# When a planner frees PSUM banks, how it ranks additions, and where three small loads are issued, in a float32 stack of attention and MLP blocks

## The chip, the cores and the metric

One core of one Trainium2 chip runs the whole program. The metric is device time in microseconds (us), the median of several executions; smaller is better. A profile is one further execution, with every instruction's start and length.

## The reference, cut to what matters

Everything is float32. `x` is 4 x 512 x 512 (four batches of 512 tokens, width 512), the context is 4 x 64 x 512. Four blocks follow one another; cut down:

```
x = x + cross_attention(ln(x), ctx)          # L0, twice: 16 heads of 128, one extra key/value each
x = x + gelu(ln(x) @ w_fc1 + b) @ w_fc2 + b  # L0's MLP, inner width 2048
x = x + alpha * (softmax(x wq (ctx wk)^T / sqrt(512)) (ctx wv)) wo        # L1
h = concat(ctx, x);  a = attention(q=x, kv=h, mask on the ctx part)       # L2, 16 heads of 32
x = x + mlp(rmsnorm(a @ out_w + out_b + x))
x = x + attention(ln(x), ctx, mask) @ cproj_w + b                         # L3, 16 heads of 32
x = x + mlp(ln(x))
```

`alpha` is one number, L2's mask is 4 x 64 int32, L3's mask is 4 x 64 bool. Neither mask is trivial to the program: each becomes an additive term (`mterm2`, `mterm3`) that is 0 or a very large negative number.

## The kernel before, in words

**No instruction's place is written by hand.** The builder functions (`l0_keys`, `l0_values`, `l0_attention`, `mlp`, `l2_attention` and so on) only describe operations to a `Plan`: which engine or engines could do each (`pe`, `dve`, `act`, `pool`, `either` = ACT or DVE, `added` = DVE or POOL), a duration estimated from the element count, and which buffers it reads and writes. `Plan.issue` then works out one order for each engine, before anything runs, and emits the instructions in it. On the chip each engine goes through its own list strictly in order; an instruction that waits for a semaphore holds everything behind it on its engine.

**Memory.** SBUF has one arena of 24 blocks, PSUM eight banks of 512 columns; a `Buf` gets its place when the plan starts the operation that first writes it, and gives it back when the last user in the plan has ended. Constants are "held" buffers with a fixed place. Names in the profile: `arena` is any SBUF buffer, `banks` any bank.

**How the work is split.** The matrix products follow a seven-product scheme (Strassen-Winograd): a 2 x 2 block product is made by seven products instead of eight, with additions of operands before (`moving_sums`, `stationary_sums`, `pair_sums`, `token_sums`, `width_sums`) and of results after. The additions before are `added` operations, one line in the profile (L1048), on DVE or POOL. The results are taken out of the banks by DVE or ACT ("evictions"): L1108 (`plus` of the MLP's first product), L1147 and L1154 (sums of the second), L938 (`plus` in L0's attention), L575/L576 (plain copies on ACT/DVE), L1594 (the exponential of L2's scores, read straight from four banks by ACT), L1388, L1404, L1676. A matmul into a bank must wait until the eviction of what was there is done.

**The order (`merge`, then `attempt`).** Work is recorded in thirteen regions, and in each two or three streams run beside each other (for instance one pair's MLP beside another pair's attention). `merge` interleaves them: `PACES` has for each stream 17 numbers; number k says where the stream should stand, in per cent of the region, when k/16 of its TensorE work is gone, and the stream with the lowest number goes next. This gives each operation a number `n` and a position `pos` (TensorE time before it). `attempt` is a list scheduler over estimated time: whenever an engine is free, it takes from that engine's heap the ready operation with the lowest `n`, if its buffers fit and its `pos` is not further than `AHEAD` (loads: `AHEAD_LOAD`) past the oldest unfinished one. ACT prefers an operation that needs no other activation table, unless one that does is over 6 us earlier in position. An eviction's bank is free, in the plan, at the very moment the eviction ends; its dependents are ready `AFTER` = 0.06 us later, or `AFTER_PE` = 0.2 us after TensorE, plus `BEFORE_PE` = 0.1 us for a TensorE operation.

**The start.** Ahead of the plan, ACT's queue issues the DMAs of `cols` and `alpha` (L663, L665), POOL's the two masks, each broadcast to 128 partitions (L668, L670). All loads of the plan go through SP's queue (L701), in the planned order. L2's context part makes `mterm2` from `mk_i`; L3's makes `mterm3` from `mk_b`; L1's attention uses `alpha` as a scalar.

Line numbers that the text uses further: L717 the products of context and weights (`mm4`), L877 the pair products of `l0_values`, L933 L0's score products, L1089 the MLP's seven products, L1367 the half-width seven products, L1571 L2's scores (four 32-row products into four banks), L1628 the transposes of their exponentials, L1763 the last transposes, before the store.

Of the kernel before, what the change touches and what calls it, by code (L numbers as in the profile page):

```python
# [18 lines left out]
P = 128  # L19
# [58 lines left out]
class View:  # L78
# [5 lines left out]
    def __init__(self, buf, key=None, path=()):  # L84
        self.buf, self.key, self.path = buf, key, path
# [122 lines left out]


class Op:  # L210
    __slots__ = ("n", "pos", "engines", "calls", "wait", "next", "takes", "uses", "table", "ready", "start", "on", "load", "port")


class Plan:
# [8 lines left out]
    SHARED_DVE, SHARED_POOL = 0.45, 0.15  # L223
    BEGIN = {"PE": 1.0, "DVE": 3.0, "ACT": 3.0, "POOL": 3.2, "SP": 0.8}

    def __init__(self, sbuf, ahead, ahead_load, reserve, full, patience, near, paces):
        self.reserve, self.full = reserve, full * BLOCK
        self.sbuf = Memory(BLOCK, sbuf)
        self.psum = Memory(1024, 4)
        self.ahead, self.ahead_load = ahead, ahead_load  # L230
        self.patience, self.near, self.paces = patience, near, paces
        self.ops, self.regions = [], []
        self.pos = 0.0

# [70 lines left out]
    def merge(self):  # L305
# [68 lines left out]
        for n, op in enumerate(merged):  # L374
            op.n, op.pos = n, pos
            pos += op.engines.get("PE", 0.0)

    def order(self):


        self.merge()
        waits = [op.wait for op in self.ops]
        left = {id(b): (b, b.left) for op in self.ops for b in op.uses}
        narrow = []
        while True:
            for op, n in zip(self.ops, waits):
                op.wait = n
            for b, n in left.values():
                b.left, b.at = n, None
            self.sbuf.reset()  # L390
            self.psum.reset()
            out, at = self.attempt(narrow)
            if out:
                return out
            width = 100 + 100 * sum(lo <= at <= hi for lo, hi in narrow)
            if width > 1500:
                raise RuntimeError(f"no room at {at}: {self.sbuf.free}, {self.psum.free}")
            narrow.append((at - width, at + 50))

    def attempt(self, narrow):  # L400
        heaps = {e: [] for e in ("PE", "DVE", "ACT", "POOL", "SP")}
        free_at = dict(self.BEGIN)
        table = None
        dma_free = 0.0
        port_busy = False
        events = [(at, 0, -1) for at in free_at.values()]
        heapq.heapify(events)
# [1 line left out]
        begun = [False] * len(self.ops)  # L409
        oldest = 0  # L410
        now = 0.0
        out = []
        busy = dict.fromkeys(heaps, 0.0)

        def arm(op):
            for e in op.engines:
                heapq.heappush(heaps[e], (op.n, op))

        for op in self.ops:
            op.ready = 0.0  # L420
# [3 lines left out]
        while left:  # L424
            progress = True
            while progress:
# [8 lines left out]
                for e, heap in heaps.items():  # L435
# [3 lines left out]
                    choice = None  # L439
                    second = None  # L440
                    while heap and len(skipped) < 60:
                        n, op = heapq.heappop(heap)
                        if begun[n]:
                            continue
                        skipped.append((n, op))
                        if op.ready > now + 1e-9:
                            continue
                        if op.pos > limit + (ahead_load if op.load else ahead):
                            break
                        room = True  # L450
                        for m in (self.sbuf, self.psum):
                            need = [b for b in op.takes if b.mem is m and b.at is None]
# [13 lines left out]
                            continue  # L466
                        choice = op
                        break
                    if second is not None and (choice is None or choice.pos > second.pos + 6.0):
                        choice = second  # L470
                    for n, op in skipped:
                        if op is not choice:
                            heapq.heappush(heap, (n, op))
                    if choice is None:
                        continue
                    op = choice
# [31 lines left out]
            now = events[0][0]  # L508
            while events and events[0][0] <= now + 1e-9:
                _, kind, n = heapq.heappop(events)  # L510
                if kind != 1:
                    continue
                op = self.ops[n]
# [2 lines left out]
                for b in op.uses:  # L516
                    b.left -= 1
                    if b.left == 0:
                        b.mem.give(b)
                for o in op.next:  # L520
                    o.wait -= 1
                    at = now + (self.AFTER_PE if op.on == "PE" else self.AFTER)
# [125 lines left out]
def stack(nc, const, sbuf, psum, a, out):  # L648
# [12 lines left out]
    nc.gpsimd.memset(eps[:, 1:2], 1e-6)  # L661
    cols = const.tile([P, NCOL], FP, name="cols")
    nc.scalar.dma_start(out=cols, in_=a["cols"])  # L663
    alpha = const.tile([P, 1], FP, name="alpha")
    nc.scalar.dma_start(out=alpha, in_=a["alpha"].to_broadcast([P, 1]))  # L665

    mk_i = const.tile([P, B * T], I32, name="mk_i")
    nc.gpsimd.dma_start(out=mk_i, in_=a["mask_i"].to_broadcast([P, B * T]))  # L668
    mk_b = const.tile([P, B * T], U8, name="mk_b")
    nc.gpsimd.dma_start(out=mk_b, in_=a["mask_b"].to_broadcast([P, B * T]))  # L670
    pl = Plan(BLOCKS, AHEAD, AHEAD_LOAD, RESERVE, FULL, PATIENCE, NEAR, PACES)
    sb, ps = pl.sb, pl.ps
    ctxT = pl.held(const.tile([P, NC * B * T], FP, name="ctxT")).v(NC, B * T)
    mterm2, mterm3 = (pl.held(const.tile([P, B * T], FP, name=f"mterm{i}")).v(B, T) for i in (2, 3))

    def col(name, i=None):
        lo, hi = _COL_AT[name]
# [6 lines left out]
    def dve(n):  # L684
        return pl.op(DVE=t_dve(n))
# [801 lines left out]
    def l2_context():  # L1487
# [4 lines left out]
            o.tensor_copy(apart[:, :256].k(0), row[:, :256])  # L1492
        with pool(256) as o:
            o.tensor_tensor(apart[:, 256:].k(1), row[:, 256:], row[:, :256], ALU.subtract)
        with dve(256) as o:
            o.tensor_scalar(mterm2, mk_i.rearrange("p (b s) -> p b s", b=B), 0.0, -3.0e38, ALU.is_equal, ALU.mult)
        bias_steps("L2_xattn_q_b")
        bias_steps("L2_k_b")
        shared2.update(row=apart, ckT=context_keys(2, "L2_k_b"), cv=context_values(2, row))
# [188 lines left out]

    def l3_context():
        row = load_row("L3_xattn_v_b")  # L1690
        with dve(256) as o:
            o.tensor_scalar(mterm3, mk_b.rearrange("p (b s) -> p b s", b=B), 0.0, LOWEST, ALU.is_equal, ALU.mult)
        bias_steps("L3_xattn_q_b")
        shared3.update(ckT=context_keys(3, "L3_xattn_k_b"), cv=context_values(3, row))

# [122 lines left out]
    g = {}  # L1818

    def a0():  # L1820
        l1.append(l1_project())
        l2_context()

# [5 lines left out]
    def a3(pair):  # L1829
# [18 lines left out]


BLOCK, BLOCKS = 8 * KW, 24  # L1850
AHEAD, AHEAD_LOAD, RESERVE = 170.0, 90.0, 2
FULL = 24


PATIENCE, NEAR = 7.0, 37.0

PACES = [
    [
        [2, 7, 11, 22, 33, 23, 51, 60, 57, 66, 72, 60, 77, 83, 93, 101, 104],
        [-4, 6, 18, 24, 27, 26, 37, 42, 48, 66, 62, 76, 74, 81, 86, 92, 97],  # L1860
        [-1, 1, 14, 14, 28, 38, 37, 50, 54, 53, 61, 74, 76, 83, 90, 96, 111],
    ],
    [
        [-1, 8, 26, 23, 26, 28, 35, 43, 60, 61, 72, 61, 72, 72, 77, 79, 88],
        [18, 28, 34, 25, 39, 34, 60, 34, 55, 62, 73, 70, 77, 98, 92, 102, 111],
    ],
    [
        [4, 13, 16, 19, 27, 36, 40, 46, 37, 58, 68, 63, 67, 76, 86, 86, 87],
        [-8, 1, 9, 15, 22, 26, 34, 41, 50, 52, 51, 64, 71, 73, 83, 88, 95],
        [-1, -2, 3, -2, 8, 6, 38, 42, 54, 74, 71, 76, 81, 88, 93, 111, 109],  # L1870
    ],
    [
        [-13, -5, 2, 16, 27, 26, 31, 24, 39, 48, 49, 55, 57, 63, 80, 95, 109],
        [-4, 10, 18, 19, 26, 43, 41, 56, 54, 61, 73, 73, 75, 94, 91, 95, 96],
    ],
    [
        [2, 5, 12, 19, 16, 36, 37, 50, 47, 54, 62, 79, 73, 80, 89, 96, 103],
        [1, 5, 12, 14, 24, 28, 38, 46, 54, 59, 62, 82, 84, 87, 84, 83, 86],
        [8, 24, 24, 32, 38, 48, 51, 61, 68, 60, 49, 62, 89, 97, 102, 104, 100],
    ],  # L1880
    [
        [-7, 9, 23, 34, 46, 63, 48, 45, 55, 75, 68, 63, 82, 78, 104, 102, 107],
        [7, 19, 26, 39, 37, 54, 56, 60, 54, 51, 76, 75, 68, 86, 97, 115, 120],
    ],
    [
        [-44, -40, -30, -8, -3, -1, 6, 16, 25, 16, 30, 43, 49, 54, 65, 75, 84],
        [-2, 4, -1, 16, 22, 37, 57, 53, 60, 67, 60, 77, 83, 62, 66, 81, 87],
        [-2, 11, 20, 17, 33, 50, 47, 53, 57, 49, 65, 77, 75, 89, 89, 98, 101],
    ],
    [  # L1890
        [-1, 4, 8, 6, 10, 20, 39, 44, 34, 44, 64, 44, 54, 60, 70, 67, 84],
        [2, 8, 10, 10, 36, 41, 64, 77, 76, 77, 84, 100, 109, 83, 90, 85, 106],
    ],
    [
        [-3, -10, 13, 23, 31, 33, 19, 44, 51, 56, 63, 67, 66, 74, 84, 102, 115],
        [23, 10, 19, -11, 18, 26, 41, 50, 50, 48, 52, 54, 63, 67, 76, 82, 87],
    ],
    [
        [3, 7, 13, 19, 24, 29, 34, 39, 45, 54, 63, 69, 74, 79, 85, 91, 97],
        [0, 6, 13, 19, 25, 31, 39, 45, 51, 57, 64, 69, 75, 81, 88, 94, 100],  # L1900
    ],
    [
        [-6, 0, 7, 12, 17, 22, 30, 36, 43, 49, 57, 63, 67, 73, 77, 85, 93],
        [-2, 3, 11, 19, 25, 31, 38, 44, 51, 56, 63, 69, 75, 81, 88, 94, 93],
        [0, 12, 13, 19, 24, 29, 35, 51, 45, 41, 49, 57, 76, 80, 83, 93, 96],
    ],
    [
        [-17, 8, 2, -1, 6, 42, 42, 48, 16, 18, 42, 59, 81, 93, 90, 99, 103],
        [-6, -5, 5, 15, 26, 36, 50, 40, 46, 53, 42, 53, 64, 80, 85, 84, 99],
    ],  # L1910
    [
        [-30, -33, -25, -10, 17, 3, 23, 46, 59, 48, 56, 45, 58, 65, 76, 73, 82],
        [-14, -3, 8, -8, 25, 53, 31, 5, 5, 26, 40, 52, 63, 75, 74, 54, 76],
    ],
]

# [55 lines left out]
```

## Time and profile before

| what | value |
|---|---|
| median of 3 runs | 2750.61 us (2749.08 to 2750.61) |
| the profiled execution | 2748.76 us, span of its instructions 2747.0 us |
| TensorE (PE) busy | 2701.2 us, 98% |
| VectorE (DVE) busy | 2044.7 us, 74% |
| GpSimd (POOL) busy | 1323.0 us, 48% |
| ScalarE (ACT) busy | 931.5 us, 34% |
| granted TensorE clock | 1.000 |
| DMA | 164.06 MB, mean 60 GB/s |

How to read the views. The page gives busy time of each engine and the costliest groups of instructions: line, engine, operation, output<-input, shape and count, then busy time, mean length of one in ns, and the idle time of the engine just before them with what ended it. The wait table says who waited for whom. The table by stretch gives each engine's busy time in a stretch of the span. In the time-ordered list a row is: start, us, engine, line, operation, count, and in brackets the idle time before it and what ended that. Matmuls are pipelined and their ends are modelled, so a matmul's row can cover up to about 0.2 us in which TensorE in fact stood still; distances between the starts of matmuls are the surer measure.

### The profile page before, as it was taken

What the parts mean: (1) busy time and instruction counts of PE and PEld (TensorE: products, weight loads), DVE (VectorE), ACT (ScalarE), POOL (GpSimd) and SP (SyncE); (2) the same over time, 40 slices, a digit from 0 to 9 for tenths busy, and PEclk for the clock granted to TensorE, in tenths of its full rate; (3) what the DMA queues carried; (4) which work ended last, traced back from release to release, by engine and by line L of the source; (5) the groups of instructions that cost most, each with busy time, mean ns of one, the idle gap of its engine ahead of it and who ended that gap; (6) DMA issues with size and microseconds to landing.
All of it is one profiled execution on the core that took longest, in us unless ns stands there. A gap on an engine that the chain in (4) does not pass through costs nothing. (4 is left out here: it accounts for less than half of the span.)

```text
span 2747.0 us, 34916 instructions
## 1 busy us (share of the span) xinstructions
PE 2701.2 (98%) x12012; PEld 1648.4 (60%) x12012; DVE 2044.7 (74%) x3661; ACT 931.5 (34%) x1759; POOL 1323.0 (48%) x1465
## 2 busy tenths in 40 slices
PE   8999999999999999999999999999999999999999
PEld 6877778788854455556555665555544545454444
DVE  6788778786864577776787678687877878878655
ACT  3223242142331114453463255154523223333211
POOL 5567576574842262333335232424745485646421
PEclk9999999999999999999999999999999999999999
DMA  7222423243121020010102011110211120202200
GB/s 242 84 89 81 131 77 115 64 134 93 50 62 57 16 69 20 20 59 14 44 25 88 8 31 45 56 32 24 70 50 35 41 67 20 58 8 84 77 16 31
DMA packets 230368, 164.06 MB, mean 60 GB/s; under 512 B 9088, under 2 KB 198656, under 8 KB 230192
## 3 DMA queue, kind: packets, MB, share of 16 engines
q1 hardware_dynamic: 229824, 161.52, 19.4%
q8 instruction: 96, 1.57, 0.2%
q14 instruction: 80, 0.66, 0.1%
q0 software_dynamic: 80, 0.16, 0.0%
q10 hardware_dynamic: 288, 0.15, 0.0%
HBM read 157.60 MB, written 4.19 MB: 59 GB/s over the span
## 5 line engine op out<-in xcount | busy, mean ns | idle before, releaser
L1048 POOL TENSOR_TENSOR arena<-arena 128x256 f32<-128x256 f32 (+4 forms) x1016 | 1064.1, 1064 | 970.5 <-DVE arena L576 169.8
L1089 PE MATMUL banks<-arena 128*128 128x512 f32 x2688 | 1201.9, 594 | 7.9 <-DVE arena L1108 2.6
L1089 PEld LDWEIGHTS banks<-arena 128*128 128x128 f32 x2688 | 497.8, 190 | 578.3 <-issue 497.6
L1048 DVE TENSOR_TENSOR arena<-arena 128x256 f32<-128x256 f32 (+4 forms) x664 | 574.1, 879 | 89.9 <-POOL arena L1048 24.8
L575 ACT COPY arena<-banks 128x512 f32<-128x512 f32 (+4 forms) x563 | 280.5, 516 | 793.9 <-PE banks L1089 196.3
L1367 PE MATMUL banks<-arena 128*128 128x256 f32 x1792 | 408.3, 380 | 3.2 <-DVE arena L938 1.5
L1367 PEld LDWEIGHTS banks<-arena 128*128 128x128 f32 x1792 | 336.2, 190 | 79.8 <-issue 21.9
L576 DVE COPY arena<-banks 128x512 f32<-128x512 f32 (+2 forms) x353 | 213.1, 613 | 160.2 <-PE banks L1089 52.5
L1124 ACT ACTIVATE arena<-arena,cols 128x512 f32<-128x512 f32 x192 | 138.0, 722 | 313.2 <-DVE arena L1048 172.9
L1108 DVE TENSOR_TENSOR arena<-banks,arena 128x512 f32<-128x512 f32 x240 | 163.8, 685 | 90.6 <-PE banks L1089 76.2
L933 PE MATMUL banks<-arena 128*128 128x260 f32 x896 | 212.0, 385 | 0.3 <-DVE arena L938 0.2
L1594 ACT ACTIVATE arena<-banks,arena 128x512 f32<-128x512 f32 x256 | 174.7, 687 | 95.1 <-DVE arena L1584 49.5
L933 PEld LDWEIGHTS banks<-arena 128*128 128x128 f32 x896 | 163.5, 188 | 36.0 <-ACT arena L575 3.0
L1582 DVE TENSOR_REDUCE arena<-banks 128x1 f32<-128x512 f32 x256 | 167.5, 681 | 13.3 <-PE banks L1571 12.2
L717 PE MATMUL banks<-ctxT,arena 128*128 128x128 f32 (+1 forms) x1152 | 164.1, 292 | 12.1 <-DMA arena<-in_L_wv 6.5
L717 PEld LDWEIGHTS banks<-ctxT,arena 128*128 128x128 f32 x1152 | 148.8, 194 | 29.5 <-issue 11.2
L1628 PEld LDWEIGHTS banks<-ident,arena 128*128 128x128 f32 x1024 | 116.5, 141 | 81.6 <-issue 35.1
L1628 PE MATMUL banks<-ident,arena 128*128 128x128 f32 x1024 | 140.9, 276 | 3.5 <-ACT arena L1594 2.9
L717 PE MATMUL banks<-arena 128*128 128x512 f32 (+2 forms) x432 | 140.4, 482 | 0.0
L1147 DVE TENSOR_TENSOR arena<-banks,arena 128x512 f32<-128x512 f32 x144 | 98.2, 685 | 50.2 <-PE banks L1089 50.1
L1605 POOL TENSOR_TENSOR arena<-arena 128x256 f32<-128x256 f32 x64 | 39.5, 617 | 188.6 <-DVE arena L1584 160.2
L717 PEld LDWEIGHTS banks<-arena 128*128 128x128 f32 x432 | 72.4, 191 | 68.3 <-issue 65.7
(155 smaller groups left out, 2528.4 us busy)
## 6 DMA issues: line engine op xcount, KB each, us to landing
arena<-in_L_w SPq DMA_DIRECT2D x192, 256.0 KB, 3.3
arena<-in_L_wk SPq DMA_DIRECT2D x80, 256.0 KB, 4.9
arena<-in_L_wv SPq DMA_DIRECT2D x64, 256.0 KB, 5.6
arena<-in_L_wqT SPq DMA_DIRECT2D x64, 256.0 KB, 5.5
arena<-in_L_wo SPq DMA_DIRECT2D x64, 256.0 KB, 5.7
arena<-in_L_wq SPq DMA_DIRECT2D x32, 256.0 KB, 3.3
arena<-in_L_wo SPq DMA_DIRECT2D x8, 1024.0 KB, 5.4
arena<-in_L_wv SPq DMA_DIRECT2D x6, 1024.0 KB, 5.7
```

The lines of the kernel that those rows point to most:

```text
L575: "ACT": lambda e, out, in_: e.copy(out, in_),
L576: "DVE": lambda e, out, in_: e.tensor_copy(out, in_),
L717: o.matmul(dst, lhs(c), rhs(c), start=(c == 0), stop=(c == NC - 1))
L933: o.matmul(p[:, : 2 * KP], lhs(c), rhs(c, b % 2), start=(c == 0), stop=(c == 1))
L1048: o.tensor_tensor(out, x, y, op)
L1089: o.matmul(p.v(), lhs(c), rhs(c), start=(c == 0), stop=(c == 1))
L1108: o.tensor_tensor(t.v(), p.v(), y.v(), ALU.add)
L1124: o.activation(g[f].v(), src.v(), func, bias=col(b1, q * NC + f))
L1367: o.matmul(p[:, i * 256 : (i + 1) * 256], lhs(c), rhs(c), start=(c == 0), stop=(c == 1))
L1582: o.tensor_reduce(m[:, i : i + 1].k(i), banks[i].v(), AX.X, ALU.max)
L1594: o.activation(y.v(), banks[i].v(), AF.Exp, bias=nm[:, i : i + 1].k(i), scale=qs, accum_out=sums[:, i : i + 1].k(i),)
L1628: o.transpose(p[:, c * P : (c + 1) * P], e[i][:, c * P : (c + 1) * P], ident)
```

## The change

Six edits.

1. `alpha`, `mk_i` and `mk_b` are no longer loaded ahead of the plan by ACT's and POOL's queues. They become held buffers, and three `load` operations of the plan (SP's queue): `alpha` first in `a0`, `mk_i` in `l2_context`, `mk_b` in `l3_context`.
2. A buffer is given back not when its last user ends but 0.06 us later (0.2 us after TensorE), and 0.1 us later still if it is a bank.
3. Heaps are ordered by a new `key`. For TensorE operations, loads and everything that touches a bank it is `pos`, as before in effect. For the others, additions above all, it is a due time: the position of the earliest TensorE operation that depends on it, less the shortest estimated duration of each operation in between plus 0.1; at most `pos` + 200.
4. An operation that is too far ahead is passed over (`continue`) where the search ended before (`break`).
5. The plan assumes that no load starts before 1.5 us; the 6 us of ACT's table choice get a name (`SWITCH`, still 6).
6. `AHEAD` 170 to 195, `AHEAD_LOAD` 90 to 112, `RESERVE` 2 to 4, `FULL` 24 to 23, `NEAR` 37 to 35, and all of `PACES` is new.

No operation on TensorE, DVE, ACT or POOL is added or removed, apart from the DMA issues.

```diff
@@ merge
+        due = [1e9] * len(merged)
+        for op in reversed(merged):
+            at = op.pos if "PE" in op.engines else 1e9
+            for o in op.next:
+                at = min(at, due[o.n])
+            if "PE" not in op.engines:
+                at -= min(op.engines.values()) + 0.1
+            due[op.n] = at
+            held = any(b.mem is self.psum for b in op.uses)
+            op.key = op.pos if held or op.load or "PE" in op.engines else min(at, op.pos + 200)
@@ attempt
-        dma_free = 0.0
+        dma_free = 1.5
...
-                heapq.heappush(heaps[e], (op.n, op))
+                heapq.heappush(heaps[e], (op.key, op.n, op))
...
                         if op.pos > limit + (ahead_load if op.load else ahead):
-                            break
+                            continue
...
+                if kind == 2:
+                    freed[n].mem.give(freed[n])
                 if kind != 1:
                     continue
...
                     if b.left == 0:
-                        b.mem.give(b)
+                        at = now + (self.AFTER_PE if op.on == "PE" else self.AFTER)
+                        if b.mem is self.psum:
+                            at += self.BEFORE_PE
+                        heapq.heappush(events, (at, 2, len(freed)))
+                        freed.append(b)
@@ stack
-    alpha = const.tile([P, 1], FP, name="alpha")
-    nc.scalar.dma_start(out=alpha, in_=a["alpha"].to_broadcast([P, 1]))
-
-    mk_i = const.tile([P, B * T], I32, name="mk_i")
-    nc.gpsimd.dma_start(out=mk_i, in_=a["mask_i"].to_broadcast([P, B * T]))
-    mk_b = const.tile([P, B * T], U8, name="mk_b")
-    nc.gpsimd.dma_start(out=mk_b, in_=a["mask_b"].to_broadcast([P, B * T]))
+    mk_i, mk_b = (pl.held(const.tile([P, B * T], t, name=f"mk{i}")) for i, t in ((2, I32), (3, U8)))
+    alpha = pl.held(const.tile([P, 1], FP, name="alpha")).v()
@@ l2_context, l3_context, a0
+        load(mk_i.v(), a["mask_i"].to_broadcast([P, B * T]), 256)
...
+        load(mk_b.v(), a["mask_b"].to_broadcast([P, B * T]), 256)
...
+        load(alpha, a["alpha"].to_broadcast([P, 1]), 8)
@@ constants; the first region of PACES (its streams: keys, values, tokens)
-AHEAD, AHEAD_LOAD, RESERVE = 170.0, 90.0, 2
-FULL = 24
-PATIENCE, NEAR = 7.0, 37.0
+AHEAD, AHEAD_LOAD, RESERVE = 195.0, 112.0, 4
+FULL = 23
+PATIENCE, NEAR, SWITCH = 7.0, 35.0, 6.0
...
-        [2, 7, 11, 22, 33, 23, 51, 60, 57, 66, 72, 60, 77, 83, 93, 101, 104],
-        [-4, 6, 18, 24, 27, 26, 37, 42, 48, 66, 62, 76, 74, 81, 86, 92, 97],
-        [-1, 1, 14, 14, 28, 38, 37, 50, 54, 53, 61, 74, 76, 83, 90, 96, 111],
+        [24, 27, 32, 17, 8, 28, 41, 52, 53, 58, 62, 74, 78, 84, 86, 88, 97],
+        [4, -12, 18, 34, 39, 40, 43, 49, 70, 55, 50, 40, 47, 98, 107, 111, 98],
+        [6, 11, 10, 5, 15, 30, 46, 48, 62, 75, 86, 97, 91, 95, 97, 103, 120],
```

## The prediction, as put on record before the changed kernel ran

> **What bounds the kernel.** I read the page's busy times first, then the table by stretch, then TensorE's wait table, then, around the longest waits, the time-ordered list.
>
> ```profile
> PE 2701.2 (98%) x12012; PEld 1648.4 (60%) x12012; DVE 2044.7 (74%) x3661; ACT 931.5 (34%) x1759; POOL 1323.0 (48%) x1465
> ```
> ```profile
> 0.00:68.00 68.00, 56.30 (x347) 43.91 (x348) 43.82 (x97) 22.67 (x43) 36.93 (x70) 1.00 0.80 245
> 68.00:2679.00 2611.00, 2582.51 (x11499) 1575.35 (x11498) 1960.21 (x3508) 899.75 (x1702) 1273.13 (x1388) 1.00 0.19 56
> 2679.00:2747.00 68.00, 62.42 (x169) 29.17 (x167) 40.68 (x57) 9.10 (x14) 12.94 (x8) 1.00 0.08 31
> ```
>
> TensorE is the bound and the change removes none of its work, so only its standstills can go. First number after a stretch's length is PE: idle is 11.7 us in the first stretch, 28.5 in the middle, 5.6 at the end, 45.8 in all. This is not the whole, because busy rows hide short stops. So I took the starts of successive matmuls: without a stop they lie 429 ns apart (128x512), 222 (128x260), 216 (128x256), 109 or 112 (128 columns); 1.07 us for the eight instructions of L1571. Summed over all instructions this dense spacing gives 2632 us. Between the first and last start there is 103 us more: some 47 us in about 540 gaps of 40 to 150 ns, which stand at changes of shape and at late weight loads and which I leave alone, and **54.8 us in 90 stalls above 150 ns**. With 6.5 us before the first matmul and 4.9 after the last start, the 54.8 are all that an order can win: 2%.
>
> What ends the stalls, in the wait table (total, times, longest):
>
> ```profile
> PE banks L717 <- DMA arena<-in_L_wk: 4.6, 1, 4.6
> PE banks L1571 <- ACT arena L1594: 4.5, 5, 1.7
> PE banks L1628 <- ACT arena L1594: 2.9, 5, 0.8
> PE banks L1089 <- DVE arena L1108: 2.6, 3, 1.2
> PE banks L1367 <- DVE arena L938: 1.5, 3, 1.0
> PE banks L1089 <- DVE arena L1048: 1.5, 2, 1.1
> ```
>
> L1108 and L938 are evictions: TensorE waited for a bank, not for data. Waits on additions themselves (L1048) are few. Why the evictions are late shows in DVE's list ahead of one of these waits (TensorE waits 1.18 us, until 2569.09, for the eviction at 2568.34):
>
> ```profile
> 2563.46 0.69 DVE L1108 TENSOR_TENSOR arena<-banks,arena 128x512 f32<-128x512 f32 x1
> 2564.49 3.74 DVE L1048 TENSOR_TENSOR arena<-arena 128x512 f32<-128x512 f32 x3 [0.34 <-POOL arena L1048]
> 2568.34 0.69 DVE L1108 TENSOR_TENSOR arena<-banks,arena 128x512 f32<-128x512 f32 x1
> ```
>
> Three additions stand ahead of the eviction. The 90 stalls by what ended them: 23 (14.7 us) by a DVE operation with an L1048 directly before it or one further back, 19 (10.6 us) by other DVE operations, 30 (16.3 us) by ACT (exponentials and copies), 16 (8.0 us) without a releaser that the profile shows, the DMA of wk (4.9 us), one by POOL (0.3).
>
> **The parts, and the sum.** It is made against the profiled execution, span 2747.0, which lies 1.8 us below its own time 2748.76 and 3.6 below the runs' median 2750.61; I apply the difference to the median.
>
> *Masks and alpha.* POOL loses two issues (0.71 and 0.55 us, L668 and L670), ACT one (0.53), and 0.16 MB leave the start. Nobody waits for them there: POOL's next work with a wait stands idle 0.82 us for `cols` anyway, ACT's first use waits for DVE. SP gets three more issues of 0.38 to 0.5 us; it is the only thing in SP's queue that is new, and behind them stand weight loads whose consumers come much later (DMA share 0.19 in the middle). Their readers, `mterm2` and `mterm3` on DVE, are asked for by scores of later stages. Taken: 0. If that cover were gone, a DVE queue would stand behind the mask's landing, 3 to 6 us by the page's landing times, once or twice. In the other direction: 0.16 MB at the 350 GB/s of the stretches from 8 to 48 us is 0.46 us off the first landing. Bounds: -0.5 to +6.
>
> *The start.* PE waits 6.50 us for the first wv, works 2.05, waits 4.64 for wk. Between the two SP issued rows and four x. By the new paces, values (4, falling to -12 at 1/16) go until their number passes 6, ahead of tokens (6) and keys (24): about 0.1 of that stream, the products of two heads. So the second wv should come before the x. A 256 KB load takes 0.75 us at 350 GB/s; with one wo between, it can land some 1.5 to 2.5 us after the first, at about 9, instead of the wk at 13.19. Then 2 us of L717 and 2 us of L877 fill TensorE until 13; x comes three loads (2.3 us) later and may leave a new gap. DMA runs full until 50 us, but then falls to 2 GB/s while PE works on, so loads are ahead and the gain isn't given back. Bounds 0 to -5.1 (all of 4.64 + 0.49); I take -3.
>
> *Additions by due time.* In the heap an addition for a product far ahead had the lower number and went before an eviction; with a due time it goes after. That touches the 23 stalls, 14.7 us. Some stand behind additions that are due themselves, and additions last 0.69 to 1.76 us on DVE in this trace, so that some collisions remain: half, -7. Bounds 0 to -14.7; the price in the other direction is the second rival's.
>
> *Banks back later.* In the plan a bank now returns 0.06 + 0.1 us later. On the chip nothing waits longer for this; the plan only stops putting a matmul where it would have stood 0.16 us. For the 72 stalls ended by DVE or ACT that is at most 72 x 0.16 = 11.5; most of them last 0.3 us or more, because DVE ran late or ACT loaded a table, which this edit doesn't see. Taken -3, bounds 0 to -11.5.
>
> *Paces and limits.* What they are worth can't be read from before. Stretches differ: from 750 to 1050 us (MLP beside little else) the gaps beyond dense spacing sum to 0.9 us, from 1050 to 2000 (L2's attention) to 46, and the worst 50 us (1900 to 1950) hold 6.8. A new mix can lose one or two such stretches, or win them. Taken 0, bounds -10 to +10. The end (from the last L1089 to the last store, 9.6 us, 0.93 of it a wait) I leave.
>
> Sum: -3 - 7 - 3 = **-13 us: 2750.6 - 13 = 2737.6**, some 0.5%.
>
> **A rule against it.** The rows first:
>
> ```profile
> L1048 DVE TENSOR_TENSOR arena<-arena 128x512 f32<-128x512 f32 x262 | 274.4, 1055 | 38.8 <-ACT arena L1124 16.6 <-POOL arena L1048 10.1 <-DMA arena<-in_L_wv 2.8
> L1108 DVE TENSOR_TENSOR arena<-banks,arena 128x512 f32<-128x512 f32 x240 | 163.8, 685 | 90.6 <-PE banks L1089 76.2 <-PE banks L1628 4.5 <-PE banks L717 3.0
> L1048 POOL TENSOR_TENSOR arena<-arena 128x512 f32<-128x512 f32 x330 | 480.7, 1467 | 404.8 <-DVE arena L576 118.9 <-ACT arena L1124 92.3 <-ACT arena L575 29.2
> ```
>
> The same addition lasts 685 ns on DVE with one operand in a bank and 1055 with both in SBUF, up to 1.76 in the stretch shown earlier. The Trainium skill (SBUF — State Buffer, section "Who interferes with whom") says that a DVE instruction with two SBUF inputs shares a read port with GpSimd reads and that the second to start blocks until the first is done. By it a due addition can be late by a whole POOL instruction, where the plan adds 0.45 us on DVE; each late one would cost up to 1.0 us more than planned, and ten of them would eat the gain of this part. The sum above doesn't use this.
>
> **Rivals.**
> *1. The stalls only move.* Evictions come sooner, but the order's slips go to additions, or to ACT: 16.3 us of stalls end on ACT, and none of the rules changes its exponentials or its table loads (89 of 1.28 us). For it: DVE keeps 74% and the same total. Against: slack on DVE is 700 us, and the 23 stalls have one clear cause. Time: 2750.6, within 5.5.
>
> *2. Additions too late: slower.* The due time subtracts the shortest estimate, DVE's 0.69 + 0.1 for 128x512, but POOL takes most of them (330 against 262) and needs 1467. Each is 0.68 late on POOL, in a chain of three (t1, t2, t4) up to 2. The place is the first of the seven products on t2 or t4 in L1089. There are 672 two-product steps there. From 19 late by 0.68 us the gain of 13 is gone, from 27 the kernel is slower by 0.2%; 32 give +21.8 - 13 = +9: 2759. Against: due times only rank; an idle engine still starts early, and POOL is idle half of the time.
>
> *3. More of it.* The new mix also spreads L2's scores, and half of the 54.8 goes: -27, 2723. For it: 30 stalls on ACT in one stage. Against: no named rule aims at ACT.
>
> *4. It doesn't do what it says:* new paces change each order anyway, so the rules' own effect drowns. Its time is rival 1's.
>
> **Numbers.** Forecast (-6 to -20) 0.45; rival 3 (below -20) 0.22; rivals 1 and 4 together 0.17; rival 2 0.16. A difference of about 0.2% (5.5 us) is what a measurement of this kernel can tell from none. Faster 0.67, same 0.17, slower 0.16. The range leaves out the far half of rival 2 (0.08) and the far third of rival 3 (0.08): 2718 to 2757; the parts' lower bounds (-5, -15, -12) also end at 2719.
>
> **What would show it.** Right: PE's wait for L1108, L938, L1147 shorter, with evictions ahead of additions in DVE's list; second product before 10 us; stalls above 150 ns at some 42 us; L1048 still the same 1680 instructions. Wrong: new rows "PE L1089 <- L1048" of several us (rival 2), ACT's rows grown (rival 1), or a stage from 1050 to 2000 that loses clearly less (rival 3) or more (paces).

## The result, and the profile after

The changed kernel takes **2721.4 us** (2719.46 to 2721.76), the kernel before 2749.9 in the same comparison: ratio 0.9895, 95% interval 0.9878 to 0.9912, 28.5 us less. The profiled execution has 2721.76 us and a span of 2720.0, 27.0 under that of before. 13 us were forecast; the time is that of rival 3 (2723).

The page of the changed kernel, busy time by engine:

```profile
PE 2685.2 (99%) x12012; PEld 1649.7 (61%) x12012; DVE 2032.4 (75%) x3675; ACT 904.6 (33%) x1715; POOL 1347.8 (50%) x1489
```

Its table by stretch (length, then PE, PEld, DVE, ACT, POOL busy, clock, DMA share, GB/s):

```profile
0.00:68.00 68.00, 60.86 (x370) 46.92 (x371) 47.57 (x104) 21.14 (x40) 40.36 (x76) 1.00 0.70 219
68.00:2652.00 2584.00, 2561.66 (x11476) 1573.55 (x11475) 1943.47 (x3511) 874.01 (x1661) 1291.51 (x1402) 1.00 0.19 57
2652.00:2720.00 68.00, 62.65 (x169) 29.24 (x168) 41.31 (x60) 9.46 (x15) 15.96 (x12) 0.98 0.11 39
```

TensorE has the same 12012 matmuls. Its idle time in the three stretches is 7.1, 22.3 and 5.4 us, after 11.7, 28.5 and 5.6. Its busy time has fallen too, by 16 us with the same work: this is stopped time that the rows of the matmuls had covered. The measure that doesn't hide it, distances between the starts of matmuls against dense spacing (2632 us in both), splits the 27.0 us:

| us | before | after | difference |
|---|---|---|---|
| start of the first matmul | 6.5 | 5.4 | -1.1 |
| 90 (now 59) stalls over 150 ns | 54.8 | 39.3 | -15.5 |
| 541 (now 440) gaps of 40 to 150 ns | 47.5 | 38.6 | -8.9 |
| smaller gaps, and after the last start | 6.2 | 4.7 | -1.5 |

By time: the excess over dense spacing falls from 13.2 to 9.3 us in the first 100 us, from 25.3 to 16.6 between 100 and 800 (L0's attention), from 46.3 to 38.7 between 1000 and 2000 (L2's attention), from 18.5 to 12.8 after. No stage owns the gain.

Who TensorE waits for now (its wait table; lines have moved: L731 was L717, L1103 L1089, L1122 L1108, L1643 L1628, L1609 L1594, L1062 L1048):

```profile
PE banks L1643 <- ACT arena L1609: 8.7, 8, 2.5
PE banks L731 <- DMA arena<-in_L_wv: 6.4, 2, 5.4
PE banks L1103 <- DVE arena L1122: 3.5, 3, 1.8
PE banks L1381 <- DVE arena L952: 0.4, 1, 0.4
PE banks L1381 <- DVE arena L1062: 0.2, 1, 0.2
```

The wait for wk is gone, the waits for wv at the start are 5.43 and 1.01 us. Of the evictions, L952 (was L938) has all but left the table, L1122 (was L1108) has not: it stands at 3.5 us after 2.6. And the longest entry is now L2's exponential on ACT, which no rule aims at: 8.7 us, where the prediction's table has 4.5 and 2.9.

One of these eight waits costs more than its row says. In TensorE's list eight transposes take 1.97 us right after it, and eight of the same line 1.10 us a little later:

```profile
1860.80 1.97 PE L1643 MATMUL banks<-ident,arena 128*128 128x128 f32 x8 [2.52 <-ACT arena L1609]
1864.53 1.10 PE L1643 MATMUL banks<-ident,arena 128*128 128x128 f32 x8
```

The table by stretch gives the reason, in its third number from the end: for this stretch the granted clock of TensorE is 0.50.

```profile
1860.80:1864.20 3.40, 3.40 (x16) 2.08 (x16) 2.79 (x7) 2.37 (x7) 0.61 (x1) 0.50 0.00 0
```

In the kernel before, whose profiled execution has a mean clock of 1.000, there is no such stretch. Here it costs at most half of 3.4 us. (The 0.98 at the end of the table above is the clock after the last matmul.)

The group of additions, by shape, DVE and POOL:

```profile
L1062 DVE TENSOR_TENSOR arena<-arena 128x512 f32<-128x512 f32 x248 | 260.4, 1057 | 38.0 <-ACT arena L1138 14.9 <-POOL arena L1062 9.6 <-ACT arena L592 5.8
```
```profile
L1062 POOL TENSOR_TENSOR arena<-arena 128x512 f32<-128x512 f32 x344 | 498.1, 1460 | 414.9 <-DVE arena L593 123.9 <-ACT arena L1138 91.1 <-DVE arena L1062 41.9
```

1057 and 1460 ns, after 1055 and 1467: an addition costs what it cost, 1680 of them in all as before. Only places in the order have changed.

### The profile page after: what moved, and what is told of

Its sections match the earlier page's. It is cut to its first block, busy times and chain, and to the rows that moved or that the text cites. A ratio compares the mean times of both kernels' runs of the same rounds, so it can differ in the third digit from the quotient of the medians.

```text
span 2720.0 us, 34911 instructions
## 1 busy us (share of the span) xinstructions
PE 2685.2 (99%) x12012; PEld 1649.7 (61%) x12012; DVE 2032.4 (75%) x3675; ACT 904.6 (33%) x1715; POOL 1347.8 (50%) x1489
## 4 chain that ended last, share of the span: by engine, by line
PE 89%; DVE 5%; POOL 2%; issue 1%; ACT 1%; DMA 0%; SPq 0%; POOLq 0%; DVEq 0%; ACTq 0%
PE banks L1103 37%; PE banks L1381 14%; PE banks L731 10%; PE banks L947 7%; PE banks L1643 4%; PE banks L1586 2%; PE banks L891 2%; PE banks L1673 2%; PE banks L826 2%; POOL arena L1062 2%; DVE arena L1062 2%; PE banks L1557 1%; PE banks L1434 1%; PE banks L1052 1%; PE banks L776 1%
## 5 line engine op out<-in xcount | busy, mean ns | idle before, releaser
L1062 POOL TENSOR_TENSOR arena<-arena 128x256 f32<-128x256 f32 (+4 forms) x1042 | 1094.9, 1068 | 904.9 <-DVE arena L593 187.2
L1103 PE MATMUL banks<-arena 128*128 128x512 f32 x2688 | 1196.9, 594 | 4.2 <-DVE arena L1122 3.5
L1103 PEld LDWEIGHTS banks<-arena 128*128 128x128 f32 x2688 | 498.7, 190 | 587.0 <-issue 522.2
L1062 DVE TENSOR_TENSOR arena<-arena 128x256 f32<-128x256 f32 (+3 forms) x638 | 551.2, 877 | 71.5 <-POOL arena L1062 23.4
L592 ACT COPY arena<-banks 128x512 f32<-128x512 f32 (+3 forms) x528 | 265.2, 519 | 783.9 <-PE banks L1103 254.7
L593 DVE COPY arena<-banks 128x512 f32<-128x512 f32 (+4 forms) x388 | 230.8, 605 | 160.6 <-PE banks L1103 50.0
L1122 DVE TENSOR_TENSOR arena<-banks,arena 128x512 f32<-128x512 f32 x240 | 163.1, 685 | 94.2 <-PE banks L1103 87.5
L1609 ACT ACTIVATE arena<-banks,arena 128x512 f32<-128x512 f32 x256 | 174.2, 686 | 99.8 <-DVE arena L1599 75.2
L731 PE MATMUL banks<-ctxT,arena 128*128 128x128 f32 (+1 forms) x1152 | 161.8, 291 | 7.0 <-DMA arena<-in_L_wv 6.4
L1643 PEld LDWEIGHTS banks<-ident,arena 128*128 128x128 f32 x1024 | 117.1, 141 | 78.1 <-issue 29.8
L731 PEld LDWEIGHTS banks<-ctxT,arena 128*128 128x128 f32 x1152 | 147.6, 194 | 26.6 <-issue 8.4
L1643 PE MATMUL banks<-ident,arena 128*128 128x128 f32 x1024 | 138.4, 276 | 8.8 <-ACT arena L1609 8.7
L731 PE MATMUL banks<-arena 128*128 128x512 f32 (+2 forms) x432 | 141.0, 482 | 0.3 <-DVE arena L1161 0.3
L731 PEld LDWEIGHTS banks<-arena 128*128 128x128 f32 x432 | 72.8, 191 | 68.5 <-issue 66.0
```

What stands on the lines that cost most here:

```text
L592: "ACT": lambda e, out, in_: e.copy(out, in_),
L593: "DVE": lambda e, out, in_: e.tensor_copy(out, in_),
L731: o.matmul(dst, lhs(c), rhs(c), start=(c == 0), stop=(c == NC - 1))
L1062: o.tensor_tensor(out, x, y, op)
L1103: o.matmul(p.v(), lhs(c), rhs(c), start=(c == 0), stop=(c == 1))
L1122: o.tensor_tensor(t.v(), p.v(), y.v(), ALU.add)
```

## The experiments

Three theories stood at first. **R**: the rules themselves make the gain, as the prediction has it. **P**: the new paces do. **F**: paces are found by a search under certain rules and fit only these. Later two came for what a search is worth. **S**: searching longer is enough. **H**: the plan's own estimate must be honest, so that a search has something true to lower.

That estimate is the end of the last operation in the plan's reckoning (`now` when `attempt` ends), in us. It is worked out when the kernel is built, and is no time of the chip. It is 2705.6 for before and 2700.8 for the changed kernel.

In the table below, "late banks" is edit 2 of the change, "due key" edit 3, and "searched" are numbers found by the searches described further on. Each ratio is against the kernel before in the same comparison, where its median was 2749.5 to 2751.3. For each kernel I counted two things in the trace. *Tight banks*: gaps of 40 to 150 ns between matmuls where a weight load (this matmul's, or that of the one before) started less than 60 ns ahead of its matmul, and within 130 ns after a DVE or ACT instruction that reads a bank set the semaphore it waits for. *Behind additions*: stalls over 150 ns ended by a DVE operation other than an addition that has an L1048 directly before it or one further back in DVE's list.

| kernel | late banks | due key | paces | median us | ratio to before (95%) | span | estimate | span over it | tight banks | behind additions, us |
|---|---|---|---|---|---|---|---|---|---|---|
| before | no | no | old | 2749.9 | 1 | 2747.0 | 2705.6 | 41 | 154 | 13.2 |
| old_plus_masks_inside | no | no | old | 2762.0 | 1.0031 to 1.0065 | 2758.5 | 2730.1 | 28 | 171 | 11.6 |
| old_plus_due_key | no | yes | old | 2752.3 | 1.0000 to 1.0019 | 2750.5 | 2720.1 | 30 | 151 | 6.2 |
| old_rules_new_paces | no | no | new | 2756.6 | 1.0017 to 1.0036 | 2752.1 | 2713.1 | 39 | 181 | 12.8 |
| new_no_late_banks | no | yes | new | 2748.2 | 0.9983 to 1.0002 | 2746.9 | 2707.2 | 40 | 166 | 9.7 |
| old_rules_refitted | no | no | searched | 2745.9 | 0.9979 to 0.9998 | 2741.1 | 2699.6 | 41 | 173 | 10.5 |
| due_key_only_refitted | no | yes | searched | 2738.9 | 0.9943 to 0.9972 | 2736.8 | 2694.8 | 42 | 168 | 10.1 |
| old_plus_late_banks | yes | no | old | 2747.9 | 0.9985 to 1.0003 | 2748.4 | 2728.4 | 20 | 117 | 4.1 |
| new_rules_old_paces | yes | yes | old | 2755.0 | 1.0004 to 1.0023 | 2751.7 | 2734.9 | 17 | 108 | 6.7 |
| new_no_due_key | yes | no | new | 2744.7 | 0.9967 to 0.9989 | 2740.1 | 2720.7 | 19 | 112 | 13.4 |
| late_banks_only_refitted | yes | no | searched | 2735.2 | 0.9928 to 0.9957 | 2733.4 | 2712.0 | 21 | 85 | 8.3 |
| new_rules_refitted_from_old | yes | yes | searched | 2737.4 | 0.9938 to 0.9972 | 2735.5 | 2714.8 | 21 | 101 | 12.1 |
| new_masks_ahead | yes | yes | new | 2725.8 | 0.9896 to 0.9925 | 2723.7 | 2703.0 | 21 | 76 | 7.0 |
| new_banks_later | 0.16 more | yes | new | 2738.9 | 0.9946 to 0.9976 | 2737.3 | 2726.2 | 11 | 87 | 4.4 |
| changed kernel | yes | yes | new | 2721.4 | 0.9878 to 0.9912 | 2720.0 | 2700.8 | 19 | 86 | 7.1 |

**The rules without the numbers.** The changed kernel with `AHEAD` to `PACES` of before:

```diff
-AHEAD, AHEAD_LOAD, RESERVE = 195.0, 112.0, 4
+AHEAD, AHEAD_LOAD, RESERVE = 170.0, 90.0, 2
...
-        [24, 27, 32, 17, 8, 28, 41, 52, 53, 58, 62, 74, 78, 84, 86, 88, 97],
+        [2, 7, 11, 22, 33, 23, 51, 60, 57, 66, 72, 60, 77, 83, 93, 101, 104],
```

> The changed kernel with the limits and paces of before: all rules of the change, none of its new numbers. Theory R (the rules make the gain, as the prediction has it): 2737 to 2742, since additions (-7) and banks (-3) stay and only the new start is lost. Theory F (fit: the numbers were found by a search under exactly these rules, and rules without fitting numbers bring nothing): no faster than before, 2745 to 2775; the plan's own estimate of its end, which the kernel computes when it is built, is 2735 here against 2701 for the changed kernel.

Measured 2755.0: all rules, and slower than before by 0.04 to 0.23%. Theory R is out. Its wait table shows where the time went, to ACT:

```profile
PE banks L1643 <- ACT arena L1609: 14.7, 16, 2.6
PE banks L1381 <- ACT arena L1495: 7.7, 4, 4.3
```

**The numbers without the rules.** The same exchange in the kernel before.

> The kernel before with the new limits and paces, all rules old. Theory R: 2744 to 2750, only the earlier second product at the start is won (-3), evictions still stand behind additions. Theory F: between, 2735 to 2755, because paces fitted to other rules lose most of their worth. If paces alone carried the gain (theory P): 2721 to 2727.

2756.6, 1.6 above the upper end of what F expected here. P is out, and F holds in the main: neither half of the change gains by itself. That both are slower than before need not be their order alone. Their profiled executions have a mean granted clock of 0.997 (before 1.000), with stretches of 0.5 as shown above; by 0.003 x 2750 us this is at most some 8 us, an estimate, and as much as they lose. The other kernels below have 0.996 to 0.998, so that differences of a few us between them may hold such a share too.

**One rule taken away.**

```diff
-                        at = now + (self.AFTER_PE if op.on == "PE" else self.AFTER)
-                        if b.mem is self.psum:
-                            at += self.BEFORE_PE
-                        heapq.heappush(events, (at, 2, len(freed)))
-                        freed.append(b)
+                        b.mem.give(b)
```

> The changed kernel, but buffers are given back in the plan at the moment the last user ends, as before. Theory R: 2724 (3 us of the gain are the banks'). Theory F: some 10 us slower, 2728 to 2740: the plan again counts on banks that are not there, and the small gaps of 40 to 150 ns in the L0 stage come back (440 of them now, 541 before).

2748.2, worse than either expected: with this rule gone nearly all of the gain goes. Tight banks double, from 86 to 166.

```diff
-            op.key = op.pos if held or op.load or "PE" in op.engines else min(at, op.pos + 200)
+            op.key = op.pos
```

> The changed kernel, but heaps ordered by position for all operations, so additions are taken in order of their record again. Theory R: 2728 (7 us of the gain are the additions'), with stalls behind additions back at some 14 us. Theory F: 2735 to 2750; the plan's own estimate rises by 20 us.

2744.7, as F said. Stalls behind additions are back at 13.4 us, as R said, but the loss is 23 us, not 7.

**One rule added to before.** The reverse of these two edits; the second brings edit 4 with it (operations too far ahead are passed over).

> The kernel before with one rule added: buffers are given back 0.06 (after TensorE 0.2) us late, banks 0.1 more. Theory R: 2747 (-3). Theory F: the paces no longer fit, 2745 to 2775; the stalls that the plan now knows of are avoided, but the numbers are of another order.

> The kernel before with one rule added: additions ranked by due time (and operations too far ahead passed over). Theory R: 2743 (-7), stalls on an eviction behind an addition halved from 13 us. Theory F: 2745 to 2770.

2747.9 and 2752.3: no gain that can be told from none, and a kernel as fast as before or up to 0.2% slower. The first time fits R (2747) as well as F, the second fits F alone. Yet both rules do in the trace what they say: tight banks fall from 154 to 117 under the first, stalls behind additions from 13.2 to 6.2 us under the second. (They fall even further, to 4.1, under the first, which has no due key: this count is not a measure of that rule alone.) What was won came back elsewhere: under the second, stalls that end on ACT's exponential or copies rise from 16.2 to 22.9 us, and the wait table of the first begins its waits for ACT with

```profile
PE banks L1634 <- ACT arena L1600: 11.4, 16, 2.5
PE banks L1373 <- ACT arena L1487: 5.5, 1, 5.5
```

**Masks and alpha alone,** taken out of the changed kernel, and put into before.

```diff
-        load(mk_i.v(), a["mask_i"].to_broadcast([P, B * T]), 256)
+    nc.gpsimd.dma_start(out=mk_i, in_=a["mask_i"].to_broadcast([P, B * T]))
... (the same for mk_b, and for alpha on ACT's queue)
```

> The changed kernel with the masks and alpha loaded ahead of the plan by POOL's and ACT's queues, as before. By the DMA reading: first product 0 to 1 us later, all else equal: 2721 to 2723. Theory F: three loads less on SP shift the whole list of the plan after them, so that the order is another one: 2721 to 2740 without any one place to show for it.

> The kernel before with the masks and alpha loaded inside the plan, nothing else. By the DMA reading: 2749 to 2750, the first product up to 1 us sooner. Theory F: slower, 2755 to 2775, as an unfitted order of the same work; this run measures what any small disturbance of the fitted order costs.

The first matmuls of three kernels, in TensorE's list by time: before (masks ahead), before with masks inside, changed with masks ahead. The idle time in brackets is what to compare.

```profile
6.50 2.05 PE L717 MATMUL banks<-ctxT,arena 128*128 128x128 f32 x8 [6.50 <-DMA arena<-in_L_wv]
```
```profile
5.52 2.05 PE L712 MATMUL banks<-ctxT,arena 128*128 128x128 f32 x8 [5.52 <-DMA arena<-in_L_wv]
```
```profile
6.20 2.05 PE L736 MATMUL banks<-ctxT,arena 128*128 128x128 f32 x8 [6.20 <-DMA arena<-in_L_wv]
```

The changed kernel starts at 5.43. So the masks' broadcasts cost the first product 0.8 to 1.0 us. But the totals move otherwise: some +4 us in the changed kernel (the two intervals overlap), and before with this small edit becomes 12 us slower, with 13.7 us more in stalls over 150 ns (68.5 for 54.8; one of them is a wait of 6.2 us for ACT). This is what F expected: a disturbed order, whose numbers were found for another, can cost ten us and more wherever it happens to fall. The plan itself saw both: its estimate rises by 2.2 in the changed kernel, by 24.5 in the other.

**Searching again.** Limits and paces were changed at random, and a change was kept if the estimate did not rise. First under all old rules, starting from the new paces, until the estimate was as low as that of the changed kernel:

```diff
-AHEAD, AHEAD_LOAD, RESERVE = 170.0, 90.0, 2
+AHEAD, AHEAD_LOAD, RESERVE = 196.1452, 96.1624, 4
...
-        [2, 7, 11, 22, 33, 23, 51, 60, 57, 66, 72, 60, 77, 83, 93, 101, 104],
+        [24, 34, 34, 17, 8, 28, 41, 52, 53, 58, 62, 74, 78, 84, 86, 88, 97],
```

> The kernel before, all rules old, with paces found by a further search on the plan's own estimate, starting from the new paces: estimate 2700, as low as that of the changed kernel (2701). If searching alone made the gain (theory S), the chip should give about 2721. If the rules make the estimate true (theory H, honest estimate: kernels with banks given back late ran 17 to 21 us over their estimate so far, those without 28 to 41), it should give 2735 to 2742, with over 150 gaps in which a weight load starts right after an eviction (154 before, 86 after), and 13 us of stalls behind additions.

2745.9: 4 us for an estimate that promised 6, and a span 41 us over it as before; the median is even somewhat above H's 2742. S is out for the old rules. Stalls behind additions are 10.5 us, not 13. The same with late banks another 0.16 us later, without a search:

```diff
-                            at += self.BEFORE_PE
+                            at += self.BEFORE_PE + 0.16
```

> The changed kernel, banks given back another 0.16 us later in the plan (0.32 in all), numbers not searched again; nothing on the chip waits longer by it. Theory H: gaps with a weight load right after an eviction fall further, from 86 to 40 to 70, and the chip stays some 10 to 20 us over the plan's estimate, which is 2726 here: 2736 to 2746, slower than the changed kernel, because the order no longer fits. Theory R: 2718 to 2724, more of the same.

2738.9, as H said. But tight banks stay at 87, where 40 to 70 were expected: a second 0.16 us takes no more of them than the first. Now each rule with a search of its own, and all rules with a search from the old numbers:

```diff
-AHEAD, AHEAD_LOAD, RESERVE = 195.0, 112.0, 4
+AHEAD, AHEAD_LOAD, RESERVE = 213.9750, 107.2468, 4
...
-        [24, 27, 32, 17, 8, 28, 41, 52, 53, 58, 62, 74, 78, 84, 86, 88, 97],
+        [23, 26, 31, -1, -9, 28, 41, 52, 53, 51, 62, 74, 65, 84, 86, 88, 92],
```

> The changed kernel without late banks, its numbers searched again under that rule: the plan's own estimate is 2695, lower than that of the changed kernel (2701). Theory S (searching makes the gain): 2712 to 2718. Theory H (the estimate must know of late banks): 2730 to 2740, with 150 or more gaps in which a weight load starts right after an eviction, and stalls behind additions at some 7 to 10 us, as the due key gives them.

> The changed kernel without due key, its numbers searched again under that rule: the plan's estimate is 2712, 11 above the changed kernel's and 9 below the same without a new search. Theory H: 2728 to 2734, 11 us below the kernel without a new search (2741.9 to 2747.5), and the key's share of the gain is then some 10 us; stalls behind additions stay at 13 us. Theory S: no lower than 2735.

> All rules of the change, the numbers of before searched again under them, though not for as long: estimate 2715, was 2735 without the search. Theory H: 2730 to 2738, clearly faster than before, so that the very numbers of the change are not needed, only numbers found under true rules. If it stays at 2745 or more, the new numbers have a worth of their own that the estimate doesn't see.

2738.9, 2735.2 and 2737.4, against 2751.3 for before in the same comparison: H's expectations, the second missed by 1 us. That second time also fits S (no lower than 2735) and decides nothing; the first decides, for S wanted 2712 to 2718 there. The kernel with the lowest estimate of all, 2694.8, is 17 us slower than the changed one: without late banks it runs 42 us over its estimate. With them alone this search didn't bring the estimate below 2712, but the chip keeps to it within 21. And the old numbers, searched again under the new rules, give half of the gain, so that the very numbers of the change are not needed for a gain; whether a longer search from there gets all of it wasn't tried. Stalls behind additions went against what was expected: 8.3 us without the due key, 10.1 and 12.1 with it. They are no measure of that rule.

## Why the prediction was wrong in size

**What held.** TensorE's work is the same, only standstills went. The second product now starts at 8.49 (before 10 was forecast). Masks and alpha cost nothing where they are read: the int32 mask lands at 740 us and is read at 766, the other at 1336 and 1358. Stalls over 150 ns came down to 39.3 (42 was forecast). Hardly an addition became late: L1103 waiting for L1062 has no row in the wait table, and the longest wait for an addition is 0.9 us, once, at the last transposes, so that rival 2 found no place. The rule against it didn't bite either, and the sum was right to leave it out: additions last what they lasted. Its price is in both traces all the same. On DVE a 128x512 addition takes 690 ns where POOL does nothing meanwhile, and on average 1147 (before) and 1143 where it does; that is what the plan allows for (0.69 + 0.45).

**The step that failed: "Paces and limits. What they are worth can't be read from before. ... Taken 0".** The sum has three terms (-3, -7, -3), each as if it acted by itself on stalls seen before, and puts the new numbers at nothing. The runs show that there is no such sum. Rules without the numbers of the change give +5, numbers without the rules +6; each of the two rules alone -2 and +3; rules and numbers together -28.5. What gains is an order whose numbers fit the rules: the old numbers, searched again under the new rules, won 13.9 us. That all rows of `PACES` are new stood in the diff; how they were found isn't on record.

**Rival 3 has the time by luck.** It wanted half of the 54.8 us of long stalls to go because L2's scores are spread. The long stalls lost 15.5, L2's attention gave 7.6 of the 27 us, and the waits for its exponential didn't shrink (7.4 us in two rows, now 8.7).

**Why the search could now gain.** Seven kernels without late banks ran 28 to 42 us over their estimate, seven with them (as the change has them) 17 to 21. Kernels with nearly the same estimate show that this isn't only a low estimate's own error: at 2720 the chip is 30 us over without late banks (old_plus_due_key) and 19 with them (new_no_due_key), at 2713 to 2715 it is 39 and 21. Nor is it the clock: with half of its stretches of granted clock 0.5 (the most that they can cost) taken off each kernel, 23 to 41 us are left without late banks and 8 to 18 with them. Without the rule the excess grows as the estimate falls, from 28 at 2730 to 42 at 2695: there the estimate could be lowered by using banks that were not yet there, and the chip didn't follow. Of the 27 us of span, 4.8 are a lower estimate (2705.6 to 2700.8), and 22 are that the chip comes closer to it (41.4 over, now 19.2). Late banks by themselves turn the kernel before into an honest one (2728.4) but not a faster one. That the due key gives a search an order that it can bring lower is likely but not shown: with late banks the estimate is 2700.8 with the key and 2712.0 without, yet the search from the old numbers stopped at 2714.8 with it. That the two alone, each searched, give 12.5 and 16.2 us and the change 28.5 looks like a sum, but all three also hold the new start, the two searches began at the numbers of the change, and they were not equally long.

**The second miss: "some 47 us in about 540 gaps of 40 to 150 ns, ... which I leave alone".** They gave 8.9 of the 14 us by which the gain in span exceeds the 13 forecast, and the 54.8 us of longer stalls were not all that an order can win. More than a quarter of the gaps, 154 with 13.0 us, are banks taken at the last moment. One of them, in the list by time of the kernel before:

```profile
172.04 0.42 DVE L938 TENSOR_TENSOR arena<-banks,arena 128x260 f32<-128x260 f32 x1
172.07 1.14 PE L1367 MATMUL banks<-arena 128*128 128x256 f32 x4
172.49 0.43 DVE L1048 TENSOR_TENSOR arena<-arena 128x256 f32<-128x256 f32 x1
172.51 0.51 PEld L1367 LDWEIGHTS banks<-arena 128*128 128x128 f32 x3 [0.25 <-DVE arena L938]
```

The eviction L938 ends at 172.46, the weight load that needs its bank starts 0.05 us later, when TensorE has already come to that product. TensorE never shows as idle, for its rows overlap; but the next matmul starts 104 ns later than dense spacing. The seven kernels without late banks have 151 to 181 such gaps (12.9 to 15.3 us), the eight with them 76 to 117 (6.6 to 9.8). So in these gaps the rule's direct worth is some 6 us, the mean 14.1 less the mean 8.3. It was sized at 3, and looked for in the long stalls.

**Additions by due time: -7** was right as a count and wrong as a gain. Behind additions the stalls fell from 13.2 to 7.1 us; with the old paces and this rule alone from 13.2 to 6.2, and the kernel got no faster. One expected sign was missing too: the waits for L1122 are longer, not shorter.

**The start: -3.** Idle time in the first 68 us fell by 4.6. The bound of 0.46 us for the masks was too low: 0.8 to 1.0.

**Open.** About 6 of the 22 us by which the chip keeps closer to the plan are tight banks. Most of the rest lies in stalls over 150 ns, 15.5 us fewer in the changed kernel; by which chain each of them went is not shown. Late banks by themselves don't lower them: old_plus_late_banks has some 60 us, before 54.8. Of the 17 to 21 us by which the honest kernels still miss their estimate, 2 to 10 at most are the halved clock, which the plan doesn't know; the rest wasn't taken apart. Whether the delay counts for banks or for SBUF too wasn't tried apart, and edits 4 and 5 had no run of their own; new_no_late_banks has both and is 40 us over its estimate, so they are not what makes it honest.

## What to carry to other kernels

Where a program orders its own instructions by estimated times, and its free numbers were searched, a change of rules and a change of numbers can't be priced one by one: ask first whether the estimate has come closer to the chip, and compare span less estimate, not only spans. A small difference is no gain by itself (17 us over at 2755.0 here); it is what lets a lower estimate count. A rule that does in the trace just what it says can still move nothing, because the time comes back at the next wait; only the whole order, found again under the rule, shows its worth. And before a kernel is called bound by an engine that is 98% busy, lay the starts of its instructions beside their dense spacing: here busy rows hid more lost time than the idle time shows.

## What the runs showed of the hardware that was not expected

Where a weight load starts only when its matmul is due, the next matmul starts about 0.1 us late, though the bank was free before (104 ns in the row above; 154 such gaps in the kernel before sum to 13.0 us). A single long wait of TensorE can be followed by a halved clock: after 2.52 us for ACT the granted clock was 0.5 for 3.4 us, and eight transposes took 1.97 us instead of 1.10. And three broadcasts of 0.16 MB in all, on other queues than the weights', hold back the first weights by 0.8 to 1.0 us: the six kernels with them ahead start their first matmul at 6.2 to 6.6 us, the nine others at 5.3 to 5.7.
